# Three quarters of the feed-forward weights loaded beside the projections, the last one held back by an early logit, and the end of the first tile taken three steps at a time

## The chip, the cores and the metric

One NeuronCore of a Trainium2 chip runs the whole program. The metric is the device time of one execution in microseconds (us). A single core has no second die to compare with, so a run counts as slow only if it is over 1.5% above the fastest of the same kernel. Two runs are compared by ratio: the mean time of one kernel's fast runs over the mean of the other's fast runs of the same rounds on the same chip, with a 95% interval. That is not quite the ratio of the medians quoted beside it.

The profile names the engines PE (TensorE; PEld is its weight loads), DVE (VectorE), ACT (ScalarE), POOL (GpSimd) and SP (SyncE). A "q" behind a name (ACTq) is the issue of a DMA by that engine. "L947" is line 947 of the kernel shown. The changed kernel has more lines, so the same instruction has another number in it: the attention product is L1158 before and L1169 after, the gather L941 and L947.

## The reference, cut to what matters

```python
hs = layer_norm(h_source, ln1_scale, ln1_bias)        # h_source is x, 4096 x 512
ht = layer_norm(h_target, ln1_scale, ln1_bias)
q, k, v = ht @ Wq + bq, hs @ Wk + bk, hs @ Wv + bv    # 8 heads of 64; q scaled by 1/8
logits = where(adj != 0, q k^T, -1e30)                # adj: 4096 x 4096, about 0.4% ones
ctx = softmax(logits) @ v
ht = layer_norm(ht + ctx @ Wo + bo, ln2_scale, ln2_bias)
out = ht + gelu(ht @ W1) @ W2                         # W1 is 512 x 2048, W2 2048 x 512
return layer_norm(x + out)
```

The adjacency is sparse, some 16 neighbours to a row. The kernel therefore builds a list of neighbours per node, writes K and V to memory, and gathers the rows that a tile of 128 nodes needs.

## The kernel before

The program is written as Python generators that are woven together. The framework puts the result into one fixed order of instructions per engine at compile time. A "product" below is one attention product on VectorE, for up to three neighbours of each node of a tile; a "list block" is VectorE's work on one quarter of a tile's adjacency rows. Three stages follow each other and overlap: projections of x to K and V beside the building of neighbour lists from adjacency blocks; attention tile by tile (gathers by GpSimd, products and sums on VectorE); and the feed-forward part (FFN) of finished groups of tiles on TensorE beside the attention of later ones.

W1 and W2 are loaded in quarters. Two are loaded beside the projections. The other two come when the projections are done, into memory that the projections held:

```python
wp = mid.enter_context(tc.tile_pool(name="s1w", bufs=1, side="right"))   # holds R0, constants
...
def load_quarter(pool, q, engine=nc.sync):
    w1.append(pool.tile([P, KC, D], F32, name=f"w1_{q}"))
    w2.append(pool.tile([P, KC, D], F32, name=f"w2_{q}"))
    engine.dma_start(w1[q], W1[:, q * D:(q + 1) * D].rearrange("(c p) n -> p c n", p=P))
    engine.dma_start(w2[q], W2[q * D:(q + 1) * D, :].rearrange("(c p) n -> p c n", p=P))
...
                    if n in (8, 10):                    # pairs of projection tiles
                        load_quarter(wp2, n // 2 - 4)
...
            src.close()                                 # frees wk and wv
            mid.close()                                 # frees s1w, with the records R0
            pools = [late.enter_context(tc.tile_pool(name="s2wa", bufs=1)),
                     late.enter_context(tc.tile_pool(name="s2wb", bufs=1, side="right"))]
...
            def weights():
                for q, pool in enumerate(pools):
                    yield 10.0
                    load_quarter(pool, q + 2, nc.scalar)
```

Nodes are sorted by degree, and each node's *record* (its number, its degree, its list) is scattered to memory and read back tile by tile. Every gather needs a record; so does the output scatter, which writes a tile's finished rows to where the nodes belong. Seven buffers hold records:

```python
                rec = sp.tile([P, E0 + MAXE], I32, name="rec", bufs=7)
                eng = nc.gpsimd if i < 2 else nc.sync
                eng.dma_start(rec[:, :RW], recs_d[part][r0:r0 + P, :])
```

The end of a tile (normalising, its output matrix, the second layer norm, the transposes for the FFN) is a generator too, of which each call of `advance` takes one step, twice per group of logits:

```python
                def advance():
                    go_on()
                    for t in list(tails):
                        if next(t, StopIteration) is StopIteration:
                            tails.remove(t)
```

## Time and profile before

| | before |
|---|---|
| time, median of the first 3 runs (range) | 1874.8 us (1873.1 to 1874.85) |
| profiled execution, state fast | 1878.9 us, mean granted clock 0.960 |
| first attention product (of 211, counted from 0) | 315.8 us |
| first FFN matmul | 371.9 us |
| products 26 to 32 (from start to start) | 40.4 us |
| product 210, the last | 1739.5 us |

The prediction shows the page's shares and the table by stretch. Two further views also belong here. The first is the queue of SyncE's DMA issues by what it waited for (columns: line, releaser, us in total, times, longest). The loads of records (L955) wait again and again for an output scatter, because it is the last reader of a record's buffer:

```profile
SPq L955 <- DMA out_dram<-xt,rec: 958.9, 17, 103.8
```

The second is GpSimd's timeline around the first output scatter (start, duration, instruction; in brackets the idle time before it and what ended it):

```profile
491.28 1.03 POOL L1243 DMA_INDIRECT out_dram<-xt,rec  x1 [6.72 <-ACT xt L1239]
...
496.94 1.26 POOL L941 DMA_INDIRECT xt<-in_x_dram,rec  x1 [0.30 <-issue]
498.50 0.95 POOL L941 DMA_INDIRECT kv<-kvd,rec  x1 [0.30 <-issue]
...
511.06 0.95 POOL L941 DMA_INDIRECT tq<-in_L_gnn_h_target_dram,rec  x1 [2.70 <-PE t L1052]
```

GpSimd waits 6.72 us with the scatter, then gathers on without a stop, and fetches the rows of h_target for a later tile at 511.06, after 2.70 us of waiting. VectorE does not wait at all in that stretch: it is busy 19.98 of 20 us at 500 to 520.

### The profile page before, as it was taken

To read this page: it belongs to the slowest core of one execution; us is meant where nothing else is said; L and a number is where in the kernel's file an instruction comes from. 1 tells how busy PE (TensorE), PEld (TensorE's weight loads), DVE (VectorE), ACT (ScalarE), POOL (GpSimd) and SP (SyncE) were. 2 spreads that over 40 slices of the span, in tenths; PEclk is the share of its full clock that TensorE was granted. 3 is DMA by queue.
4 is the path that set the end of the run, shared out by engine and by line. 5 is a ranking of instruction groups with operands and counts; after the bars stand their busy time and mean duration, and the time that the engine had idled before them with its cause. 6 is when DMAs were issued, how large, how long until landed. Compare 5 with 4: busy or idle time off the path is not lost. (4 is left out here: it accounts for less than half of the span.)

```text
span 1878.9 us, 22938 instructions
## 1 busy us (share of the span) xinstructions
PE 1705.1 (91%) x7030; PEld 1100.5 (59%) x7030; DVE 1432.2 (76%) x2591; ACT 1247.5 (66%) x3139; POOL 885.2 (47%) x804
## 2 busy tenths in 40 slices
PE   7999784698998989999999989899999999999996
PEld 3444332565665656666666656566666666656664
DVE  7999855989998837787878889888777778777400
ACT  6777634577886737776777777677767677777411
POOL 1000143645445465656666666655555545655101
PEclk9999987698999989999999999999999999999998
DMA  9999958888887657777778778777677767666000
GB/s 349 381 380 360 353 167 332 314 273 299 313 271 246 207 158 230 257 252 263 251 253 276 271 269 293 241 246 246 216 239 232 248 224 237 227 220 223 23 1 24
DMA packets 147757, 463.28 MB, mean 247 GB/s; under 512 B 24468, under 2 KB 29160, under 8 KB 147624
## 3 DMA queue, kind: packets, MB, share of 16 engines
q0 software_dynamic: 95696, 342.19, 53.9%
q1 hardware_dynamic: 44112, 96.44, 14.5%
q10 hardware_dynamic: 7816, 23.08, 3.2%
q8 instruction: 58, 0.95, 0.2%
q14 instruction: 75, 0.61, 0.1%
HBM read 430.76 MB, written 30.89 MB: 246 GB/s over the span
## 5 line engine op out<-in xcount | busy, mean ns | idle before, releaser
L941 POOL DMA_INDIRECT kv<-kvd,rec x603 | 684.1, 1134 | 492.2 <-PE cps L1129 217.2
L1266 PE MATMUL pf<-h2T,w 128*128 128x256 f32 (+1 forms) x2176 | 475.9, 371 | 3.4 <-issue 2.6
L1275 PE MATMUL po<-w,gt 128*128 128x512 f32 x1024 | 469.4, 600 | 0.0
L1158 DVE TENSOR_TENSOR kv<-kv,tq 128x1536 f32<-128x1536 f32 (+2 forms) x211 | 352.6, 1677 | 107.2 <-DMA kv<-kvd,rec 84.5
L1266 PEld LDWEIGHTS pf<-h2T,w 128*128 128x128 f32 x2176 | 391.0, 193 | 68.8 <-issue 23.4
L1141 ACT ACTIVATE kv<-kv,pa 128x64 f32<-128x64 f32 x1520 | 391.5, 336 | 3.7
L1162 DVE TENSOR_REDUCE lg<-kv 128x24 f32<-128x1536 f32 (+2 forms) x211 | 351.0, 1670 | 1.8 <-ACT pa L1138 0.3
L1129 PE MATMUL cps<-ident,kv 128*128 128x128 f32 x2008 | 269.8, 282 | 52.9 <-DMA kv<-kvd,rec 20.4
L1129 PEld LDWEIGHTS cps<-ident,kv 128*128 128x128 f32 x2008 | 241.3, 146 | 129.2 <-issue 81.1
L1275 PEld LDWEIGHTS po<-w,gt 128*128 128x128 f32 x1024 | 188.3, 193 | 189.9 <-issue 189.0
L1121 DVE TENSOR_TENSOR kv<-kv,p 128x1024 f32<-128x1024 f32 (+1 forms) x211 | 249.9, 1191 | 47.4 <-ACT p L1166 30.3
L674 POOL TENSOR_TENSOR n_rs<-n_ve,mhalf 128x2 f32<-128x2 f32 (+2 forms) x51 | 51.3, 1005 | 333.8 <-DVE n_ve L667 136.7
L1269 ACT ACT_TABLE_LOAD x111 | 142.4, 1283 | 1.7
L980 PE MATMUL t<-wq,tq 128*128 128x512 f32 x256 | 119.9, 612 | 16.0 <-ACT tq L974 13.1
L906 PE MATMUL pq<-wk,h2T 128*128 128x512 f32 x256 | 124.0, 628 | 11.2 <-ACT h2T L896 5.8
L722 DVE MAX8 cand<-sg 128x8 uint16<-128x103 uint16 (+1 forms) x640 | 131.9, 257 | 0.7
L1269 ACT ACTIVATE gt<-pf 128x512 f32<-128x512 f32 x128 | 76.4, 597 | 72.5 <-PE pf L1266 60.8
L906 PE MATMUL pq<-wv,h2T 128*128 128x512 f32 x256 | 118.2, 604 | 6.0 <-ACT tq L908 5.9
L715 ACT ACTIVATE sg<-kv 128x1024 uint8<-128x1024 int32 x84 | 88.6, 1056 | 47.2 <-DVE cand L722 20.6
L1056 PE MATMUL t<-wo,rb 128*128 128x512 f32 x256 | 117.9, 604 | 1.5 <-DVE rb L1046 1.5
L906 PEld LDWEIGHTS pq<-wk,h2T 128*128 128x128 f32 x256 | 50.0, 202 | 78.2 <-issue 60.2
L1166 ACT ACTIVATE p<-lg 128x24 f32<-128x24 f32 (+2 forms) x179 | 33.7, 188 | 91.4 <-DVE lg L1162 69.9
(154 smaller groups left out, 1607.7 us busy)
## 6 DMA issues: line engine op xcount, KB each, us to landing
kv<-in_adj_dram SPq DMA_DIRECT2D x84, 512.0 KB
a<-in_adj_dram SPq DMA_DIRECT2D x44, 512.0 KB
kvd<-tq ACTq DMA_DIRECT2D x32, 512.0 KB
kv<-kvd,rec POOLq DMA_INDIRECT x603
kv<-in_L_gnn_h_target_dram SPq DMA_DIRECT2D x32, 256.0 KB
kv<-in_x_dram SPq DMA_DIRECT2D x15, 512.0 KB
rest_d<-gid SPq DMA_DIRECT2D x32, 160.0 KB
w<-in_L_gnn_W_dram SPq DMA_DIRECT2D x4, 1024.0 KB
```

Source lines behind the costliest of these rows:

```text
L722: nc.vector.max(cand[:, h * SQ + s, :], wd[:, w0:w1])
L906: nc.tensor.matmul(pkv, hT[:, kc, j * P:(j + 1) * P], w[:, kc, :], start=kc == 0, stop=kc == KC - 1)
L941: nc.gpsimd.indirect_dma_start(out=dst, out_offset=None, in_=table[:, :], in_offset=bass.IndirectOffsetOnAxis(ap=idx, axis=0))
L980: nc.tensor.matmul(pq, hT[:, kc, :], wq[:, kc, :], start=kc == 0, stop=kc == KC - 1)
L1121: nc.vector.tensor_tensor(v4, v4, p[:, j0:j0 + m, :].unsqueeze(3) .to_broadcast([P, m, H, HD]), ALU.mult)
L1129: nc.tensor.matmul(cps[:, c, :], kv[:, j, D + c * P:D + (c + 1) * P], ident, is_transpose=True, start=j0 + j == 0 and c == 0, stop=j0 + n ...
L1141: nc.scalar.mul(v, v, pa[:, hd:hd + 1])
L1158: nc.vector.tensor_tensor(kv[:, :n, :D], kv[:, :n, :D], tq[:, :D].unsqueeze(1).to_broadcast([P, n, D]), ALU.mult)
L1162: nc.vector.tensor_reduce(lg[:, :n, :], kv[:, :n, :D].rearrange("p j (h d) -> p j h d", h=H), AX.X, ALU.add)
L1266: nc.tensor.matmul(pf[:, k, :], w1[(f0 + k) // KC][:, kc, (f0 + k) % KC * P:((f0 + k) % KC + 1) * P], h2T[:, kc, :w], start=kc == 0, stop= ...
L1269: nc.scalar.activation(gt, pf, AF.Gelu_apprx_tanh)
L1275: nc.tensor.matmul(po[j], gt[:, k, j * P:(j + 1) * P], w2[(f0 + k) // KC][:, (f0 + k) % KC, :], start=False, stop=f0 + k == FC - 1, skip_g ...
```

## The change

The intent is to rid ScalarE of the wait of 14.20 us at the hand-over from projections to attention. Buffers of the early pools move into free slots of the gather ring, so that three quarters can be loaded beside the projections. The last quarter sits on wk and wv alone and is held by a logit of the second group. The end of the first tile goes three steps per call, so that its FFN starts while TensorE idles (in the kernel before it is busy 29.72 of 52 us at 320 to 372).

```diff
-            wp = mid.enter_context(tc.tile_pool(name="s1w", bufs=1, side="right"))
-            ip = mid.enter_context(tc.tile_pool(name="s1", bufs=2, side="right"))
+            words = ring[:, 7, :]                      # constants, moments (cut)
+            first_rec = ring[:, 11, :NA * RW].bitcast(I32).rearrange("p (n w) -> p n w", w=RW)
+            first_oh = ring[:, 11, 512:512 + NB * NA // 2].bitcast(BF16)
...
-            def load_quarter(pool, q, engine=nc.sync):
+            def load_quarter(pool, q, engine=nc.sync, gate=None):
...
+                if gate is not None:
+                    nc.scalar.copy(w1[q][:, 0, 0:1], gate)
+                    nc.scalar.copy(w2[q][:, 0, 0:1], gate)
...
-            DEEP = 8
+            DEEP = 7                                   # adjacency blocks ahead
...
-                return ring[:, DEEP + i // 2 % 4, i % 2 * D:(i % 2 + 1) * D]
+                return ring[:, 8 + i // 2 % 3, i % 2 * D:(i % 2 + 1) * D]
...
-                tails, pend = [], []
+                tails, pend, begun = [], [], set()
                 def advance():
                     go_on()
                     for t in list(tails):
-                        if next(t, StopIteration) is StopIteration:
-                            tails.remove(t)
+                        for _ in range(1 if h2Ts or begun else 3):
+                            if next(t, StopIteration) is StopIteration:
+                                tails.remove(t)
+                                break
+                    if h2Ts:
+                        begun.add(True)
...
+                            if k == 1:
+                                load_quarter(s2wa, NQ - 1, nc.scalar, lg[:, 0, 0:1])
...
-                    if n in (8, 10):
-                        load_quarter(wp2, n // 2 - 4)
+                    if n in (6, 8, 10):
+                        load_quarter(wp2, n // 2 - 3)
...
-            pools = [late.enter_context(tc.tile_pool(name="s2wa", bufs=1)),
-                     late.enter_context(tc.tile_pool(name="s2wb", bufs=1, side="right"))]
+            s2wa = late.enter_context(tc.tile_pool(name="s2wa", bufs=1))
...
-            def weights(): ...                         # two quarters after the projections
```

More of the change, by code (lines that the diff above doesn't have):

```diff
@@ L556, in adj_resnorm_kernel @@
             mid = ExitStack()
-            wp = mid.enter_context(tc.tile_pool(name="s1w", bufs=1, side="right"))
-            ip = mid.enter_context(tc.tile_pool(name="s1", bufs=2, side="right"))
             psi = mid.enter_context(tc.tile_pool(name="psi", bufs=1, space=PSUM))
             ring = kp.tile([P, RING, 2 * D], F32, name="kv")
+            words = ring[:, 7, :]
+            st, zero, bob, rbc = (words[:5 * KC, :P], words[:, 128:136], words[:, 136:136 + D],
+                                  words[:, 648:648 + KC])
+            mvh = words[:, 656:656 + 2 * NT].rearrange("p (n c) -> p n c", c=2)
+            veh, rsh, nmh = (words[:, 720 + i * NT:720 + i * NT + NT] for i in range(3))
+            first_rec = ring[:, 11, :NA * RW].bitcast(I32).rearrange("p (n w) -> p n w", w=RW)
+            first_oh = ring[:, 11, 512:512 + NB * NA // 2].bitcast(BF16)
             def xrows(n):
@@ L578, in adj_resnorm_kernel @@
                 nc.sync.dma_start(first_x[:, j, :], x[j * P:(j + 1) * P, :])
-            st = wp.tile([5 * KC, P], F32, name="st")
             for i, v in enumerate((ln1_scale, ln1_bias, ln2_scale, ln2_bias, bv)):
@@ L583, in adj_resnorm_kernel @@
             wv = load_w(kvw, Wv, "wv", nc.scalar)
-            Rs = [pool.tile([P, n, RW], I32, name=f"R{i}")
-                  for i, (pool, (_, n)) in enumerate(zip((wp, lp), PARTS))]
+            Rs = [first_rec, lp.tile([P, NBT, RW], I32, name="R1")]
             deg = lp.tile([P, NT], F32, name="deg")
@@ L625, in late_constants @@
             def late_constants():
-                zero = wp.tile([P, 2 * D // P], F32, name="zero")
                 nc.vector.memset(zero, 0.0)
@@ L632, in late_constants @@
                 nc.sync.dma_start(wq, Wq.rearrange("(c p) n -> p c n", p=P))
-                bob = row_bcast(wp, bo, "bob")
+                nc.sync.dma_start(bob, bass.AP(tensor=bo.tensor, offset=bo.offset,
+                                               ap=[[0, P], [1, D]]))
                 nc.sync.dma_start(bqr, bass.AP(tensor=bq.tensor, offset=bq.offset,
@@ L647, in late_constants @@
                                         ident)
-                rbc = wp.tile([P, KC], F32, name="rbc")
                 nc.vector.tensor_copy(rbc.unsqueeze(2), pt.rearrange("p (c t) -> p c t", c=KC)
@@ L688, in adj_resnorm_kernel @@
             held, moms = [], list(range(NT))
-            mvh = wp.tile([P, NT, 2], F32, name="mvh")
             adjs = []
-            DEEP = 8
+            DEEP = 7
             FILL = 5
@@ L791, in moments @@
                 t = hrow(i)
-                stats(ip, t, mvh[:, i, :], "n0")
+                stats(sp, t, mvh[:, i, :], "n2")
             def sort(part):
@@ L811, in sort @@
                 else:
-                    oh = wp.tile([P, NB * n], BF16, name="oh")
+                    oh = first_oh
                 oh = oh[:, :NB * n].rearrange("p (b i) -> p b i", b=NB)
@@ L868, in measure @@
                         return
-                    mv = ip.tile([P, G, 2], F32, name="mv")
+                    mv = sp.tile([P, G, 2], F32, name="mv2")
                     for j in range(G):
-                        stats(ip, state[n][:, j, :], mv[:, j, :], "n1")
-                    scales[n] = rstd_of(ip, mv, G, "n1")
+                        stats(sp, state[n][:, j, :], mv[:, j, :], "n2")
+                    scales[n] = rstd_of(sp, mv, G, "n2")
                 def scale(n):
@@ L1345, in prepare @@
                     moments(moms.pop(0))
-                rs, nm = rstd_of(wp, mvh, NT, "n0")
+                nc.vector.tensor_scalar_add(veh, mvh[:, :, 1], EPS)
+                nc.gpsimd.tensor_tensor(rsh, veh, mhalf, ALU.pow)
+                nc.vector.scalar_tensor_tensor(nmh, mvh[:, :, 0], -1.0, rsh, op0=ALU.mult,
+                                               op1=ALU.mult)
                 for R, (i0, n) in zip(Rs, PARTS):
                     Rf = R.bitcast(F32)
-                    nc.vector.tensor_copy(Rf[:, :, RST], rs[:, i0:i0 + n])
-                    nc.vector.tensor_copy(Rf[:, :, RST + 1], nm[:, i0:i0 + n])
+                    nc.vector.tensor_copy(Rf[:, :, RST], rsh[:, i0:i0 + n])
+                    nc.vector.tensor_copy(Rf[:, :, RST + 1], nmh[:, i0:i0 + n])
                 nm = lp.tile([P, QW], I32, name="a", bufs=2)
@@ L1369, in adj_resnorm_kernel @@
             mid.close()
-            pools = [late.enter_context(tc.tile_pool(name="s2wa", bufs=1)),
-                     late.enter_context(tc.tile_pool(name="s2wb", bufs=1, side="right"))]
+            s2wa = late.enter_context(tc.tile_pool(name="s2wa", bufs=1))
             psf = late.enter_context(tc.tile_pool(name="psf", bufs=2, space=PSUM))
-            def weights():
-                for q, pool in enumerate(pools):
-                    yield 10.0
-                    load_quarter(pool, q + 2, nc.scalar)
             def other_lists():
@@ L1384, in other_lists @@
                 yield from sort(1)
-            _weave((att, 0), (chain(feed(g) for g in range(len(GROUPS))), 0), (other_lists(), WAIT),
-                   (weights(), 0))
+            _weave((att, 0), (chain(feed(g) for g in range(len(GROUPS))), 0), (other_lists(), WAIT))
     left = nc.values_load(flag[0:1, 0:1], min_val=0, max_val=1)
```

## The prediction

> **What bounds the kernel now.** I read the busy shares by engine first, then the page's forty slices, then a table of busy times by stretch, and last the timeline of the stretch that looked thin. TensorE is busy for 91% of the span and VectorE for 76%, so the question is where TensorE is not busy, and whether what holds it there is something the change touches.
>
> ```profile
> PE 1705.1 (91%) x7030; PEld 1100.5 (59%) x7030; DVE 1432.2 (76%) x2591; ACT 1247.5 (66%) x3139; POOL 885.2 (47%) x804
> ...
> PE   7999784698998989999999989899999999999996
> ...
> PEclk9999987698999989999999999999999999999998
> DMA  9999958888887657777778778777677767666000
> ```
>
> The PE row drops to 4 and 6 tenths in slices 7 and 8 (47 us each, so 282 to 376 us), with the clock falling in slices 6 to 8. That stretch and a little before it in 20 us pieces; the columns are TensorE, its weight loads, VectorE, ScalarE and GpSimd busy us, then granted clock, DMA share and GB/s:
>
> ```profile
> 240.00:260.00 20.00, 20.00 (x61) 9.77 (x60) 18.58 (x73) 9.29 (x18) 12.13 (x12) 1.00 0.31 104
> 260.00:280.00 20.00, 14.28 (x29) 6.06 (x28) 3.52 (x16) 6.16 (x12) 9.30 (x11) 0.83 0.62 185
> 280.00:300.00 20.00, 13.49 (x31) 6.02 (x30) 8.67 (x35) 10.82 (x22) 0.00 (x0) 0.83 0.70 245
> 300.00:320.00 20.00, 5.46 (x13) 1.89 (x11) 10.37 (x27) 6.00 (x12) 11.10 (x11) 0.75 1.01 384
> 320.00:340.00 20.00, 9.00 (x39) 7.84 (x40) 19.64 (x25) 8.64 (x38) 16.03 (x14) 0.50 1.03 410
> 340.00:360.00 20.00, 14.37 (x62) 10.96 (x61) 18.74 (x21) 12.02 (x44) 13.31 (x12) 0.72 0.97 355
> ```
>
> Between 260 and 320 us nothing is full until the DMA at the end; from 320 us VectorE is full (attention on tile 0 plus lists) and TensorE half idle. So there are two stages: a hand-over from projections to attention that waits, and a VectorE-bound first attention tile. The timeline says what the hand-over waits for:
>
> ```profile
> 266.79 0.39 ACTq L573 DMA_DIRECT2D w<-in_L_gnn_W_dram  x1
> ...
> 267.28 0.58 ACT L908 COPY tq<-pq 128x512 f32<-128x512 f32 x1 [14.20 <-DMA rec<-R,ranki]
> ...
> 273.66 0.56 ACT L896 ACTIVATE h2T<-t,cols 128x256 f32<-128x256 f32 x1 [4.69 <-DMA w<-in_L_gnn_W_dram]
> ...
> 283.22 0.81 ACT L967 ACTIVATE tq<-tq,rec 128x512 f32<-128x512 f32 x1 [5.04 <-DMA tq<-in_L_gnn_h_target_dram,rec]
> ...
> 299.55 0.33 ACTq L910 DMA_DIRECT2D kvd<-tq  x1
> ...
> 299.90 0.46 ACTq L574 DMA_DIRECT2D w<-in_L_gnn_W_dram  x1
> ...
> 305.85 0.94 POOL L941 DMA_INDIRECT kv<-kvd,rec  x1 [26.39 <-issue]
> ...
> 315.82 1.76 DVE L1158 TENSOR_TENSOR kv<-kv,tq 128x1536 f32<-128x1536 f32 x1 [4.30 <-DMA kv<-kvd,rec]
> ```
>
> Read from the top: ScalarE stands for 14.2 us ahead of evicting a projection. What released it is the scatter of the records, and the first thing it did then was to issue a weight quarter. The last quarter of W1 and W2 lies on the bytes of the records R0 (pool "s1w"), so its load, issued from ScalarE in program order, holds every ScalarE instruction behind it until the scatter has read R0. Then 4.7 us more for a weight DMA. The last K/V write goes out at 299.55, quarter 2 straddles it, the first K/V gather follows at 305.85, and attention starts at 315.8.
>
> [...] the rate in this trace, 368 GB/s in the first 100 us with many transfers in flight, decides, and makes a quarter (two transfers of 1.05 MB) 5.7 us. [...]
>
> **The change part by part.**
>
> Removed: the ScalarE wait. The four projection tiles still open at 251 us write K/V at 273, 277, 290 and 300 us. By TensorE a tile costs 16 matmuls, 3.6 us per eight, and 1.2 us of transposes: 8.4 us, so four cost 34 us and would end at about 285 us instead of 299.
>
> Added: a third quarter beside the projections (at the sixth pair of tiles, about 115 us). That stage has a DMA share of 0.98 to 1.0, so its 2.1 MB are not free. The two quarters already loaded there, issued at 150.8 and 185.7 us, are each followed by a wait of the list stage for adjacency rows:
>
> ```profile
> 167.62 1.06 ACT L715 ACTIVATE sg<-kv 128x1024 uint8<-128x1024 int32 x1 [3.56 <-DMA kv<-in_adj_dram]
> ...
> 201.15 1.06 ACT L715 ACTIVATE sg<-kv 128x1024 uint8<-128x1024 int32 x1 [7.56 <-DMA kv<-in_adj_dram]
> ```
>
> Their mean, 5.6 us, is what the transfer takes, so I charge 5 us. DEEP from 8 to 7 takes one prefetched block of seven away and may make each such wait a little longer; I put that in the range. The moved buffers (records, constants, one-hot) lie in ring slots 7 and 11, which the third and fourth gather group fill long after their last reading; no new wait.
>
> When can attention start? Two chains must both end. *Records*: the scatter started at 244.5; plus 5 is 249.5; its 16 instructions took 21 us: 270.5; records back, 8 us before with a weight quarter ahead of them, 5 estimated: 275.5; two x gathers, 2.6 us, go first: 278; the h gather, 7.4 us before, say 6: 284; front end (scale 0.8, transposes 1.1, copies 1.5, eight matmuls 3.7, bias 0.7, hops between) 10 us where it took 19 among blocked evictions: 294. *Projections*: 285 plus about 2 of the DMA delay, 4 us until the last write has landed (6.3 before): 291; the first three gathers, 3.8 us to issue and 3 to land: 298. So attention starts at about 299 us, 17 us earlier than 315.8.
>
> Moved: the last quarter to ScalarE at the second group of logits, held there by two one-element copies (about 0.2 us each). It now sits on wk and wv only, which are free by then. It competes with gathers at a DMA share near 1; before, quarter 2 was moved at the same time, so the bytes after 296 us are the same, but now they come behind the first gathers instead of ahead of them. VectorE may wait up to one quarter's 5.7 us; I charge 2.
>
> Three steps at a time: tile 0's end runs from its first VectorE step to the first FFN matmul as
>
> ```profile
> 339.29 0.24 DVE L1026 SCALAR_TENSOR_TENSOR pm<-rec,p 128x88 f32<-128x88 int32 x1
> ...
> 371.86 0.80 PE L1266 MATMUL pf<-h2T,w 128*128 128x128 f32 x2
> ```
>
> 32.6 us, for twelve steps of which two are taken per group of logits. With three at a time it is four calls, two groups, or some 10 us, but the dependent work itself (four ScalarE passes, 4 us of matmuls, a 2 us power on GpSimd) is about 15 us. So the FFN of group 0 starts some 15 us sooner against attention, into a TensorE that is only 29.7 of 52 us busy at 320 to 372. That group's FFN is a single tile and the next group's cannot start before its own normalised rows exist, so the last FFN does not come earlier by this; it only takes about 15 us of TensorE work out of 372 to 440, where VectorE loses time. VectorE is busy 94.8 of 108 us at 372 to 480; I give a third of the 13 us back, 4, and take 1 for waits inside the squeezed end.
>
> Sum: 17 - 2 + 4 - 1 = 18 us, 1874.8 - 18 = 1856.8, so 1857.
>
> Does the gain last? From 480 to 580 VectorE is 99% busy, and from 700 to 1760 TensorE is busy 1012 of 1060 us: stages with no slack, in a fixed order, so they move as a block.
>
> **The rivals.** (a) *The DMA takes it back*: the early stage is bound by the DMA, and a third quarter, shallower prefetch and a late quarter among the gathers eat 12 us or more. For it: shares of 1.0 and the 7.6 us wait. Against: the share is only 0.31 at 240 to 260 and 0.62 at 260 to 280, so the delay is partly caught up there. It would give 1868 to 1875. (b) *The records become the bound*: projections finish early and attention waits for scatter and front end, as slow as before. For it: h rows landed only at 283 and the scatter starts 5 us later. This gives a start near 306 and 1864. (c) *The early FFN counts in full*: all of TensorE's idle 52 us at 240 to 400 is filled and none is lost later. For it: TensorE sets the end. Against: VectorE is full from 320 on and the FFN of group 1 waits for attention. It would give 1830 to 1838.
>
> **Range and chances.** The start of attention is uncertain by about 7 us, the two smaller terms by 4 each, later re-timing by 4: 1842 to 1868 for 8 in 10. Over 2% faster means below 1837.3, which needs (c): 0.08. Slower than 1912 needs a fresh stall that I don't see: 0.02. Within 2%: 0.90.
>
> **What would show it.** No ScalarE wait above 5 us between 250 and 285; last K/V write near 287; first attention product near 299; first FFN matmul near 340, that is 40 us after it where it was 56; an adjacency wait of 4 to 7 us after 115 us and scatter near 249. I am wrong if attention starts later than 308 (rival a or b), or if the gain at the end differs by over 8 us from that at the start of attention.

## The result, and the profile after

The changed kernel took 1891.21 us (median of 4 runs, 1890.34 to 1892.88) against 1873.95 us (1871.41 to 1874.85) of the kernel before on the same chip: ratio 1.0095 [1.0078, 1.0113]. It is about 0.9% slower, where 1% faster was predicted. Both profiled executions are of state fast, 1888.8 us at a clock of 0.961 and 1878.9 us at 0.960, so the clock explains nothing. I show the rows of the changed kernel's page that answer to those in the prediction:

```profile
PE 1701.8 (90%) x7030; PEld 1097.7 (58%) x7030; DVE 1431.7 (76%) x2591; ACT 1240.2 (66%) x3135; POOL 884.7 (47%) x804
...
PE   7999883778899989999999989999999999999996
...
PEclk9999987898989999999999999999999999999998
DMA  9999958977767556777878888867667767766000
```

The work per engine is the same within 4 us, ScalarE's within 8 (1240.2 against 1247.5); it is its place that differs. The table by stretch (columns as in the prediction) has the hand-over no shorter to speak of, and attention on tile 0 as thin as before:

```profile
240.00:260.00 20.00, 20.00 (x60) 9.78 (x59) 19.74 (x86) 12.82 (x24) 13.25 (x13) 1.00 0.48 170
260.00:280.00 20.00, 13.89 (x32) 5.82 (x31) 6.40 (x27) 5.75 (x11) 8.60 (x10) 0.91 0.61 179
280.00:300.00 20.00, 16.32 (x33) 6.80 (x34) 15.39 (x63) 12.77 (x26) 0.00 (x0) 0.84 0.74 247
300.00:320.00 20.00, 1.72 (x4) 0.38 (x2) 11.76 (x29) 8.46 (x22) 15.49 (x14) 0.67 0.94 354
320.00:340.00 20.00, 7.10 (x31) 6.33 (x32) 17.57 (x21) 7.47 (x33) 9.86 (x10) 0.50 1.03 404
```

To see where time is lost, I read from both traces when each attention product starts. The lag is the start after minus the start before, so negative is ahead:

| product | 0 | 8 | 10 | 14 | 22 | 26 | 28 | 30 | 32 | 42 | 100 | 150 | 210 |
|---|---|---|---|---|---|---|---|---|---|---|---|---|---|
| lag, us | -4.1 | -0.1 | 21.1 | 11.9 | -6.6 | -5.5 | 3.2 | 15.9 | 14.5 | 12.2 | 15.6 | 14.2 | 9.9 |

There are three events. At the start only 4 us were won. Between products 8 and 10 some 21 us go, and by product 22 they are back, with 7 us on top. Between products 26 and 32 another 20 us go (60.4 us where the kernel before took 40.4), and most of these are never paid back: from 5.5 us ahead at product 26 the kernel falls to 9.9 us behind at the last, which is the whole difference of the two profiled executions.

**The hand-over.** The timeline of the changed kernel:

```profile
265.42 0.38 SPq L1214 DMA_DIRECT2D degs<-rec  x1
...
268.34 0.33 ACTq L916 DMA_DIRECT2D kvd<-tq  x1
...
268.71 0.56 ACT L902 ACTIVATE h2T<-t,cols 128x256 f32<-128x256 f32 x1 [9.89 <-DMA degs<-rec]
...
278.38 0.81 ACT L973 ACTIVATE tq<-tq,rec 128x512 f32<-128x512 f32 x1 [1.40 <-DMA tq<-in_L_gnn_h_target_dram,rec]
...
293.35 0.33 ACTq L916 DMA_DIRECT2D kvd<-tq  x1
...
300.15 0.94 POOL L947 DMA_INDIRECT kv<-kvd,rec  x1 [26.42 <-DMA kvd<-tq]
...
311.76 1.76 DVE L1169 TENSOR_TENSOR kv<-kv,tq 128x1536 f32<-128x1536 f32 x1 [4.64 <-DMA kv<-kvd,rec]
```

The 14.2 us wait of ScalarE is gone, and 9.89 us stand in its place. What released ScalarE was the load of the degrees (`degs`), which ScalarE has no use for. That load, used only in a check at the very end, had been hoisted to here and, by the view of SyncE's waits, stood 17.6 us for the record scatter before it went out at 265.42. The K/V write of 268.34 came after it; in e3 below, with the load moved to the end, the write went out at 260.28. Why the write was held by a load whose data it does not use is not shown. So the change removed one wait for the scatter and uncovered another.

**The first stop.** With three steps per call the first FFN matmul comes at 360.93 instead of 371.86, and its work stands in TensorE's order ahead of the matmuls of tile 2's query (tiles counted from 0), which begin at 368.98 instead of 354.12. Product 9, the first of that tile, needs the query:

```profile
360.93 0.67 PE L1280 MATMUL pf<-h2T,w 128*128 128x128 f32 x4
...
368.98 3.60 PE L986 MATMUL t<-wq,tq 128*128 128x512 f32 x8
...
377.00 0.42 DVE L726 TENSOR_TENSOR sg<-sg,lio 128x512 uint16<-128x512 uint16 x1 [4.28 <-ACT sg L721]
...
381.40 0.68 DVE L988 SCALAR_TENSOR_TENSOR tq<-t,bqr 128x512 f32<-128x512 f32 x1
...
382.21 1.09 POOL L947 DMA_INDIRECT kv<-kvd,rec  x1 [12.24 <-PE cps L1140]
382.40 3.42 DVE L1169 TENSOR_TENSOR kv<-kv,tq 128x1536 f32<-128x1536 f32 x2
```

TensorE has finished these matmuls by 372.6, but VectorE finishes the query (L988) only at 381.40: its order has list blocks (L726) first, and they wait for ScalarE. GpSimd waits 12.24 us for transposes of tile 1 meanwhile, but with a gather for a later product; the rows of product 9 had been asked for by 348. VectorE does six list blocks from 360 to 382 us without one attention product. Those lists would have had to be built later anyway, which is why this stop is paid back: by product 10 the changed kernel has begun 105 blocks against 94, by product 26 both have begun 112.

**The second stop.** The 20 us stretches of both kernels, before first, with VectorE in the third pair of columns after the two of TensorE:

```profile
500.00:520.00 20.00, 18.54 (x83) 12.51 (x82) 19.98 (x45) 17.75 (x50) 11.45 (x11) 1.00 1.00 374
520.00:540.00 20.00, 19.29 (x80) 11.84 (x79) 20.00 (x45) 15.90 (x37) 9.49 (x7) 1.00 0.88 304
```

```profile
500.00:520.00 20.00, 12.14 (x49) 7.49 (x47) 11.56 (x25) 9.23 (x28) 8.67 (x10) 0.88 0.82 310
520.00:540.00 20.00, 17.11 (x61) 10.68 (x62) 17.09 (x68) 13.90 (x23) 5.75 (x6) 0.78 0.68 220
```

All engines do less in the same 20 us: TensorE 12.14 us for 18.54, VectorE 11.56 for 19.98. Here every engine waits for another, and the view of waits from 490 to 545 us of the changed kernel gives its links (us in total, times, longest):

```profile
POOL tq L947 <- PE t L1058: 12.9, 1, 12.9
ACT p L1177 <- DVE lg L1173: 10.7, 1, 10.7
POOL kv L947 <- PE cps L1140: 9.7, 4, 5.1
DVE kv L1169 <- DMA kv<-kvd,rec: 8.8, 2, 8.4
PEld t L1058 <- ACT tq L980: 8.3, 1, 8.3
```

Its beginning is seen on GpSimd:

```profile
486.49 2.12 POOL L1257 DMA_INDIRECT out_dram<-xt,rec  x1 [6.66 <-ACT xt L1253]
...
493.51 0.96 POOL L947 DMA_INDIRECT xt<-in_x_dram,rec  x1 [1.13 <-DMA out_dram<-xt,rec]
498.41 1.75 POOL L947 DMA_INDIRECT kv<-kvd,rec  x1 [3.94 <-DMA rec<-rec]
...
524.28 1.19 POOL L947 DMA_INDIRECT tq<-in_L_gnn_h_target_dram,rec  x1 [12.88 <-PE t L1058]
```

The scatter itself waits as long as before (6.66 and 6.72 us). But the gather behind the fetch of x rows now waits 3.94 us for a record, whose buffer the scatter had just read. VectorE then stands 8.44 us for a gather, ScalarE for VectorE, TensorE for ScalarE, and GpSimd, at 524.28, for TensorE. The fetch that came at 511.06 before comes 13 us later.

That fetch is for tile 7, whose first product is 36. What product 30, the first of tile 6, follows by 1 us in both kernels is its own query, here the changed kernel and then the kernel before:

```profile
521.34 1.50 ACT L980 ACTIVATE tq<-t,b1r,cols 128x128 f32<-128x128 f32 x4
538.71 0.68 DVE L988 SCALAR_TENSOR_TENSOR tq<-t,bqr 128x512 f32<-128x512 f32 x1
```

```profile
508.58 1.50 ACT L974 ACTIVATE tq<-t,b1r,cols 128x128 f32<-128x128 f32 x4
522.98 0.69 DVE L982 SCALAR_TENSOR_TENSOR tq<-t,bqr 128x512 f32<-128x512 f32 x1
```

In the changed kernel ScalarE has that step of the query behind the 10.7 us wait of the view above. VectorE's order differs too: ten list blocks begin between products 26 and 32, where the kernel before has six, and VectorE is busy 47.6 of the 60.4 us against all of the 40.4. So some 7 of the 20 us are list work moved forward, and 13 are idle. It is still a loss: from product 26 to 42 both kernels do sixteen list blocks and VectorE is busy about as long (117.1 and 116.1 us), yet the changed kernel takes 143.3 us and the one before 125.6.

### The profile page after: what moved, and what is told of

The parts are those of the page before. It is cut to its first block, busy times and chain, and to the rows that moved or that the text cites. A ratio compares the mean times of both kernels' runs of the same rounds, so it can differ in the third digit from the quotient of the medians.

```text
span 1888.8 us, 22937 instructions
## 1 busy us (share of the span) xinstructions
PE 1701.8 (90%) x7030; PEld 1097.7 (58%) x7030; DVE 1431.7 (76%) x2591; ACT 1240.2 (66%) x3135; POOL 884.7 (47%) x804
## 5 line engine op out<-in xcount | busy, mean ns | idle before, releaser
L1140 PE MATMUL cps<-ident,kv 128*128 128x128 f32 x2008 | 264.3, 280 | 59.0 <-DVE kv L1132 43.8
L681 POOL TENSOR_TENSOR n_rs<-n_ve,mhalf 128x2 f32<-128x2 f32 (+1 forms) x50 | 42.9, 859 | 330.1 <-DVE n_ve L674 123.1
L1062 PE MATMUL t<-wo,rb 128*128 128x512 f32 x256 | 124.8, 633 | 2.3 <-DVE rb L1052 2.3
```

What stands on the lines that cost most here:

```text
L1062: nc.tensor.matmul(pa, ct[:, c, :], wo[:, c, :], start=False, stop=c == KC - 1, skip_group_check=True)
L1140: nc.tensor.matmul(cps[:, c, :], kv[:, j, D + c * P:D + (c + 1) * P], ident, is_transpose=True, start=j0 + j == 0 and c == 0, stop=j0 + n ...
```

## The experiments

All ratios are to the kernel before, from the fast runs of the same rounds. "8 to 10" and "26 to 32" are us between the starts of those products in the run's profile; 10.4 and 40.4 is the kernel before. Each is read from one profiled execution, while the ratio is over all fast runs, and the two need not go together: e6 and e18 have long second stops at small ratios.

| run | base and edit | median us | ratio [95%] | product 0 | 8 to 10 | 26 to 32 |
|---|---|---|---|---|---|---|
| e1_one_step | after, one step per call | 1894.22 | 1.0088 [1.0061, 1.0115] | 313.1 | 10.4 | 58.9 |
| e2_three_only | before, three steps per call | 1879.71 | 1.0014 [1.0002, 1.0026] | 315.4 | 34.4 | 43.4 |
| e3_degs_late | after, degrees loaded at the end | 1886.93 | 1.0052 [1.0035, 1.0068] | 312.5 | 33.3 | 56.6 |
| e4_one_step_degs_late | e1 and e3 | 1894.67 | 1.0083 [1.0054, 1.0113] | 308.9 | 10.2 | 60.1 |
| e5_handover_free | e3, six records loaded by GpSimd | 1887.54 | 1.0045 [1.0028, 1.0063] | 311.4 | 32.7 | 58.8 |
| e6_eight_records | after, eight record buffers | 1878.74 | 1.0015 [0.9996, 1.0034] | 313.3 | 32.5 | 54.8 |
| e7_two_late | after, two early and two late quarters | 1892.47 | 1.0081 [1.0056, 1.0106] | 314.8 | 30.9 | 56.6 |
| e8_depth_seven | before, seven blocks ahead | 1884.19 | 1.0029 [1.0015, 1.0042] | 319.7 | 10.2 | 41.4 |
| e9_wind_first | after, first group finished early | 1893.12 | 1.0062 [1.0041, 1.0083] | 314.7 | 32.9 | 53.4 |
| e10_wind_eight | e9 and e6 | 1888.27 | 1.0041 [1.0020, 1.0063] | 314.3 | 32.2 | 51.8 |
| e11_before_eight | before, eight record buffers | 1870.75 | 0.9952 [0.9938, 0.9967] | 316.3 | 9.7 | 40.4 |
| e12_before_wind | before, first group finished early | 1876.41 | 0.9979 [0.9969, 0.9989] | 319.4 | 9.7 | 40.6 |
| e13_last_woven | after, last quarter's place as before | 1878.90 | 1.0014 [0.9997, 1.0030] | 313.1 | 22.7 | 49.4 |
| e14_last_woven_eight | e13 and e6 | 1875.52 | 0.9992 [0.9982, 1.0002] | 317.0 | 21.5 | 46.1 |
| e15_three_eight | e2 and e11 | 1877.21 | 1.0001 [0.9985, 1.0016] | 319.5 | 34.1 | 43.7 |
| e16_before_wind_eight | e12 and e11 | 1870.28 | 0.9953 [0.9936, 0.9971] | 321.9 | 10.2 | 40.5 |
| e17_last_first_logits | after, last quarter at group 0 | 1882.70 | 1.0017 [1.0004, 1.0029] | 312.0 | 30.7 | 48.3 |
| e18_last_fourth_logits | after, last quarter at group 3 | 1886.49 | 1.0045 [1.0031, 1.0059] | 315.1 | 33.3 | 58.7 |

The runs came in five jobs; the kernel before had medians between 1876.85 and 1880.40 us in them (1873.95 in the first comparison), so medians of different jobs are not compared. The changed kernel was not run again in them: its 1.0095 rests on four runs of each kernel.

### The three steps: with and without

```diff
-                        for _ in range(1 if h2Ts or begun else 3):
+                        for _ in range(1):
```

> The changed kernel with the first tile's end back at one step a call; the loads stay as changed. Squeezed-end theory (the three steps alone put first-FFN and list work ahead of tile 2's attention in the fixed engine orders, which cost 21 us at attention group 10 and some 20 us again near 500 us): groups 8 to 10 take about 10 us instead of 31, and the whole is about 1870 us, a little under the kernel before. Load theory (more bytes in the early stage, shallower prefetch, a late quarter among the gathers cost it): stays at 1888 to 1894 us.

The other way round, the kernel before with that loop alone:

> The kernel before with the three steps alone; all loads as before. Squeezed-end theory: 1885 to 1892 us, with the stop of attention at groups 8 to 12 in its trace. Load theory: 1872 to 1877 us.

Without the three steps the first stop is gone (10.4 us) and the time stays at 1.0088: the second stop is still 58.9 us. With the three steps alone the first stop is there in full (34.4 us), the second hardly (43.4), and the cost is 0.1%. So the three steps make the first stop, nearly all of it is paid back, and the loss that lasts is not theirs.

### The hand-over: one wait behind another

In the check at the end, a copy that needs the end's sums keeps the degrees' load from being hoisted:

```diff
+                    nc.vector.tensor_copy(degs[:, i0:i0 + n, 0], ok[:, i0:i0 + n])
                     nc.sync.dma_start(degs[:, i0:i0 + n, :], rec...)
```

> The changed kernel, with the load of the degrees for the final verdict tied to the end of attention by a small copy into its tile, so that it cannot be hoisted into the hand-over. Lane theory (the K/V write of the fourth tile from the end waits for the degrees' load [...], and that load waits for the record scatter): the 9.9 us ScalarE wait before 268 us goes, the last K/V write goes out at 283 to 288 instead of 293 and attention starts near 304 instead of 311.8; the end is 4 to 8 us earlier if no order changes. Rival (the true need is the records and the front end): attention starts within 2 us of 311.8.

The same with one step per call:

> Both edits together. If both theories hold: attention starts near 304, no stop at groups 8 to 12, and 1858 to 1866 us, faster than both kernels. If only the squeezed-end theory holds: about 1870. If neither: 1888 to 1894.

In e3 the K/V write of 268.34 went out at 260.28. Yet ScalarE then stood 10.51 us, now for adjacency rows:

```profile
274.15 1.06 ACT L721 ACTIVATE sg<-a 128x1024 uint8<-128x1024 int32 x1 [10.51 <-DMA a<-in_adj_dram]
```

In the changed kernel's trace such loads (L706, from 269.69) stand in SyncE's queue behind the loads of records 2 to 5 (L961, from 265.85), which go out after the 17.6 us wait for the scatter; that it is the same in e3 was the author's estimate. The next run takes these record loads off SyncE too, issuing them from GpSimd, which waits for the scatter anyway (1.76 us in e3):

```diff
-                eng = nc.gpsimd if i < 2 else nc.sync
+                eng = nc.gpsimd if i < 6 else nc.sync
```

> The changed kernel with the degrees' load tied to the end (as in the run before) and the record loads of tiles 2 to 5 issued from GpSimd instead of SyncE, so that no queue but GpSimd's holds an instruction that waits for the record scatter. Queue theory ([...] taking one away only uncovers the next): no ScalarE wait over 5 us from 255 to 276, last K/V write at 280 to 288 instead of 293, attention starts at 298 to 306. Rival (the records' own chain, scatter to record to h row to query, sets the start): attention starts at 309 to 313 as before. The end moves by no more than 8 us either way, since the second loss near 500 us is untouched.

```profile
271.06 1.06 ACT L721 ACTIVATE sg<-a 128x1024 uint8<-128x1024 int32 x1 [8.68 <-DMA a<-in_adj_dram]
...
278.46 0.81 ACT L973 ACTIVATE tq<-tq,rec 128x512 f32<-128x512 f32 x1 [6.26 <-DMA tq<-in_L_gnn_h_target_dram,rec]
```

Attention starts at 311.4 us in e5, against 311.8 with all waits in place; 8.68 us for adjacency rows and 6.26 us for the rows of h_target are there now. Three times a ScalarE wait of 9 to 14 us was taken away, and the start moved by 4 us in all. So it is not one ScalarE wait that sets it. The traces point to the fixed order in which the last projection tiles and the first query tiles share TensorE and ScalarE, the latter waiting for the record scatter; no run changed that order alone, so this is not shown. The end moved by 0.4 to 0.5% in e3 and e5, though not through the start; e4, which starts earliest (308.9), gained nothing.

### The early quarter and the prefetch depth

Two quarters beside the projections, as before, and two held by the second group's logit:

```diff
-                    if n in (6, 8, 10):
-                        load_quarter(wp2, n // 2 - 3)
+                    if n in (8, 10):
+                        load_quarter(wp2, n // 2 - 4)
...
                             if k == 1:
+                                load_quarter(wp2, NQ - 2, nc.scalar, lg[:, 0, 0:1])
```

> The changed kernel with two quarters beside the projections, at the same places as before, and two at the first logits. Byte theory (the third quarter in the full early stage costs about 5 us there): scatter 4 to 6 us earlier, attention starts 3 to 6 us earlier, and with 2 MB more behind the first logits groups 2 to 8 take up to 6 us longer; end within 5 us of the changed kernel unless the order near group 28 changes.

And `DEEP = 7` alone in the kernel before:

> The kernel before with the adjacency prefetch at seven blocks instead of eight and nothing else. If the shallower prefetch costs the early stage: scatter and start of attention 3 us or more later, 1877 to 1883 us. If not: within 2 us of the kernel before.

A second late quarter in place of the third early one changes nothing that the intervals could tell (1.0081, 56.6 us). The expectation missed: the scatter came at 249.14 instead of 243.10, and attention started 3 us later, not earlier. Since e7 both takes a quarter away early and adds one late, it does not clear the early quarter by itself; e13 below, which keeps it and stands at 1.0014, level with e2, does. `DEEP = 7` costs the kernel before 0.3% with no stop of either kind; its attention starts at 319.7 us.

### The record buffers

```diff
-                rec = sp.tile([P, E0 + MAXE], I32, name="rec", bufs=7)
+                rec = sp.tile([P, E0 + MAXE], I32, name="rec", bufs=8)
```

> The changed kernel with eight record buffers instead of seven, so that the record of the eighth tile need not wait until the first tile's output scatter has read its own. Record theory (the loss of some 20 us between attention groups 26 and 30 starts with that wait: a gather put early in GpSimd's order stands 3.9 us for it, and VectorE, ScalarE and TensorE follow in turn): groups 26 to 30 take 32 to 40 us instead of 54, and the end is 1872 to 1881 us. Rival (the stretch is slow because of the order of the engines' queues as a whole): 48 us or more, end 1888 to 1896.

> Control: the kernel before with eight record buffers. If the record wait is a cost that the change brought in: within 3 us of the kernel before. If eight buffers are simply a gain of their own, which the change had no part in: 5 us or more faster, about 1868.

Eight buffers take the changed kernel from 1.0095 to 1.0015. But the kernel before gains 0.5% by them too, and 1.0015 over 0.9952 is 1.0063: two thirds of the change's cost remain when both have eight. In the changed kernel the six products still take 54.8 us, although the wait for the record is gone. In the two profiles e6 is 6 us ahead of the changed kernel at product 32 and 13 us at the last, so about half of the gain lies there or earlier. In e11 nothing is gained by product 32 and 12 us by the last. SyncE's queue in e11, against the 958.9 us of before:

```profile
SPq L955 <- DMA out_dram<-xt,rec: 658.6, 15, 87.0
```

In the changed kernel that total is 996.0 us and in e6 996.4, no shorter, so the sum of these waits does not explain what eight buffers are worth there.

### The end of the first group, wound up early

If the place of the first output scatter is what hurts, finishing the first group at once should help:

```diff
-                if g + 1 == len(GROUPS):
+                if g in (0, len(GROUPS) - 1):
                     while ends: wind_up()
```

> The changed kernel, with the end of the first group (normalisation and output scatter) finished right after its FFN instead of step by step beside the next group's FFN; seven record buffers. In its GpSimd order the first output scatter moves from behind gather 78 to behind gather 48. Scatter-place theory (the stretch of groups 26 to 32 is lost because GpSimd stands 6.7 us at that scatter, and then at a gather for the record that the scatter frees, with the gathers of the next groups behind it): groups 26 to 32 take 40 to 45 us (61 in the changed kernel, 40 in the one before), end 1873 to 1880. Rival (the order of the other engines near there is to blame): 55 us or more there, end 1886 to 1893.

> Both repairs: first group's end finished at once, and eight record buffers. If the two losses are different waits of the record buffers (the first near 500 us, others later), they add: 1868 to 1875, at or below the kernel before; if the one contains the other, within 3 us of the better of the two.

> Control: the kernel before with the first group's end finished at once. Its stretch of groups 26 to 32 takes 40 us already, so within 3 us of the kernel before if the place of the scatter did no harm there; 5 us or more faster if it did.

> The kernel before with eight record buffers and the first group's end wound up right after its feed-forward part. If the two gains add: 0.9952 times 0.9979, ratio 0.993, 1861 to 1868 us. If they are two ways to the same 5 us: 0.995 to 0.996, level with eight buffers alone.

On the changed kernel both runs, e9 and e10, missed. In e9 the scatter moved from behind 78 gathers to behind 48 in GpSimd's order, but the six products took 53.4 and 51.8 us and the ratios were 1.0062 and 1.0041. The place of this one scatter is thus not the cause by itself. In the kernel before, the same edit gives 0.2% alone and nothing on top of eight buffers (0.9953 and 0.9952): two ways to the same gain.

### The last quarter's place

What was left untested was where the last quarter stands. First it goes back to where the kernel before has its late loads, right after the projections and without the copies that hold it; all else of the change stays:

```diff
-                            if k == 1:
-                                load_quarter(s2wa, NQ - 1, nc.scalar, lg[:, 0, 0:1])
...
+            def weights():
+                yield 10.0
+                load_quarter(s2wa, NQ - 1, nc.scalar)
```

> The kernel after, with only the last quarter's load put back where the kernel before has its late loads (issued from ScalarE right after the projections in program order, with no copy of a logit to hold it). Theory A (the place of the last quarter, at the second group of logits, re-timed the engines' orders at the 26th to 32nd attention product): those six products take 40 to 46 us, as with three steps alone, and the ratio to before is 1.001 to 1.004. Theory B (the cause lies in what stays of the change: the third early quarter, seven blocks of prefetch, buffers moved to the gather ring, one buffer less for the moments): they take 55 to 62 us and the ratio stays 1.007 to 1.011.

> The same as the run before it with eight record buffers. Theory A: level with the kernel before with eight record buffers, ratio 0.995 to 0.998. Theory B: as the kernel after with eight, ratio 1.000 to 1.003, with 50 us or more for the six products.

> The kernel before with three steps at a time and eight record buffers, nothing of the loads changed. If the three steps cost nothing at the end and the buffers' gain adds to it: ratio 0.9952 times 1.0014, 0.995 to 0.998, with 36 to 44 us for the 26th to 32nd attention product. If three steps and the shortage of record buffers act together, eight buffers would bring it below the kernel before with eight: under 0.994.

The ratio falls from 1.0095 to 1.0014, as theory A had it, level with three steps alone. The six products take 49.4 us, between what A and B expected; 11 of the 20 us are back at this spot, and from product 30 on the run is some 12 us ahead of the changed kernel. GpSimd in e13:

```profile
483.25 1.03 POOL L1254 DMA_INDIRECT out_dram<-xt,rec  x1 [0.31 <-issue]
491.96 0.97 POOL L947 DMA_INDIRECT xt<-in_x_dram,rec  x1 [7.67 <-DMA out_dram<-xt,rec]
493.24 0.94 POOL L947 DMA_INDIRECT kv<-kvd,rec  x1 [0.30 <-issue]
...
512.36 0.95 POOL L947 DMA_INDIRECT tq<-in_L_gnn_h_target_dram,rec  x1 [4.72 <-DVE kv L1169]
```

The scatter does not wait, the gather behind the x rows comes at 493.24 instead of 498.41, and the fetch that stood 12.88 us before 524.28 comes at 512.36. With eight buffers it makes 0.9992, not the 0.995 to 0.998 expected; and e15 with 1.0001 missed its 0.995 to 0.998 as well. So an eighth buffer is worth 0.8% in the changed kernel (1.0095 to 1.0015), 0.5% in the kernel before, and 0.2% or less in e13 and e2 (1.0014 to 0.9992 and 1.0001). Its worth depends on the order it meets; the reason is not shown. Compared like with like, e14 against e15, the changed loads without the hold are worth 0.1%, within the intervals.

A quarter on its way among the first gathers and an order of queues that comes out otherwise both fit so far. Two runs tell them apart. GpSimd's compiled order has the first output scatter behind 81 gathers in before, e2 and e13, and behind 78 in the changed kernel. Holding the last quarter by group 0 gives 81, by group 3 gives 78:

```diff
-                            if k == 1:
+                            if k == 0:         # e17;  k == 3 in e18
```

> The kernel after, with the last quarter held by a logit of the first group instead of the second. Its transfer starts some 5 us earlier, still among the first gathers, but in the fixed order of GpSimd the first output scatter stands behind 81 gathers, as in the kernels that do not lose time there. Theory A1 (what costs is the order of the queues that the place of this load leads to, 160 us later): ratio 1.000 to 1.004, 42 to 50 us for the 26th to 32nd attention product. Theory A2 (what costs is the hold itself, a transfer that starts while the first tiles gather): ratio 1.007 to 1.011, and 55 us or more.

> The kernel after, with the last quarter held by a logit of the fourth group. In GpSimd's order the first output scatter stands behind 78 gathers, as in the kernel after. Theory A1: the loss between the 26th and 32nd product stays, 54 us or more, ratio 1.006 to 1.011. Theory A2: as bad or worse, since the transfer comes later still; so this run tells the two apart only together with the one before it. If it is level with the kernel before (below 1.004), the place of the scatter is not what counts.

When the quarter went out, first in e17, then in e18 (in the changed kernel it was 321.64):

```profile
315.89 0.39 ACTq L583 DMA_DIRECT2D w<-in_L_gnn_W_dram  x1
```

```profile
333.92 0.39 ACTq L583 DMA_DIRECT2D w<-in_L_gnn_W_dram  x1
```

And GpSimd, again e17 first:

```profile
487.93 1.03 POOL L1257 DMA_INDIRECT out_dram<-xt,rec  x1 [0.53 <-ACT pa L1149]
...
515.91 0.95 POOL L947 DMA_INDIRECT tq<-in_L_gnn_h_target_dram,rec  x1 [6.75 <-DVE cand L728]
```

```profile
485.10 1.94 POOL L1257 DMA_INDIRECT out_dram<-xt,rec  x1 [7.83 <-ACT xt L1253]
...
520.97 0.95 POOL L947 DMA_INDIRECT tq<-in_L_gnn_h_target_dram,rec  x1 [10.82 <-DVE cand L728]
```

The same load, held the same way among the first gathers and issued 5.75 us earlier, costs 0.0017 instead of 0.0095, with 48.3 us for the six products. Issued 12 us later it brings the second stop back, 58.7 us, at the ratio 1.0045, less than expected. (The profiled executions flatter this contrast: e17's took 1879.37 us, below its median, and e18's 1891.41 us, above it.) The transfer as such is therefore not what costs: of the two transfers issued from 321.64 us on, the one whose landing is in the trace took 12.2 us, some 150 us before the stop, and the cost does not grow with the time of issue. What is left is the order of the queues that the place of the load leads to at compile time. How much of the 0.0095 that order makes is less sure: e18 has the same place of the scatter and nearly the same stop at half the cost.

## Why the prediction was wrong

- **The wait at the hand-over.** It rightly saw the 14.2 us wait, and that the change removes it. It was worth 17 us in the sum and brought 4. The record path was even better than predicted: scatter at 243.1 us (249.5 predicted), query rows at 278.4 (284). The projections path failed: the last K/V write came at 293.35 us, not 287, behind the 9.89 us wait for the degrees' load; and from the first gather to the first product it took 11.6 us (300.15 to 311.76) where 6.8 were put down. The trace of before had 10.0 there (305.85 to 315.82); I should have used it. Rival (b), records as the bound with a start near 306, came nearest in time but not in its mechanism: tile 0's query was there by 296.3 us (294 predicted), and the first K/V gather, at 300.15, was released by the last K/V write. e3 and e5 show that no single ScalarE wait set that.
- **The third early quarter.** The step charged 5 us. A wait of 4.72 us did follow that load, at 136 us, but the scatter started 1.4 us earlier than before, not 5 later: it was caught up by then. e7 and e13 give no sign of a cost at the end. The shallower prefetch, left to the range, costs the kernel before 0.3% by itself (e8), about 5 us; that it costs as much within the change is not shown. Rival (a), the DMA taking the gain back, fell for the early stage.
- **The last quarter.** It was charged 2 us, for VectorE waiting while the transfer runs. This is the mis-sized term: by e13 its place costs about 0.8% (1.0095 less 1.0014), some 15 us. The mechanism was wrong too: not the transfer beside the gathers but, by e17 and e18, the order of queues 160 us later.
- **Three steps.** Put at plus 4 less 1. The FFN did start earlier (360.93, predicted near 340), but ahead of tile 2's query in TensorE's order and with list blocks ahead of it in VectorE's, which stopped attention for 21 us. The stop was paid back in list work, so the net is 0.1% lost (e2).
- **"They move as a block."** This is the step that failed most. Attention started 4 us ahead and was still 5.5 us ahead at product 26, so the sum to there had only its sizes wrong. Then 20 us were lost in the very stretch that I called 99% busy and without slack. A stage without slack can still lose, and here it lost because the fixed orders were no longer the same orders: ten list blocks instead of six between those products, and the query of tile 6 at 538.71 us instead of 522.98. The prediction named "later re-timing by 4" as a margin; it was 20 there and 15 at the end. That the loss at the end (17 us by the medians) is about as large as the gain that was forecast is chance.

What stays open: why the scheduler puts the scatter and the fetches where it does, and which link of the new order is decisive. The scatter's place marks the slow orders (75 to 79 gathers ahead: 54.8 to 60.4 us, in the changed kernel, e1, e3 to e7 and e18; 81 or 82: 40.4 to 49.4, in the kernel before, e2, e8, e11, e13 to e15 and e17), but e9 shows that moving it alone does not cure them.

## What to carry to other kernels

Before taking a wait away, list what the same engine would wait for next: the next load behind the same event, and any late load that the engine is released by without using its data (here 14.20 us gave way to 9.89 us for the degrees, and these to 10.51 us for adjacency rows). Where a scheduler fixes the order at compile time, moving a load is two edits, the transfer and a new order for every queue; put the load at two or three neighbouring places and look at all of them before believing a cause, since here one group of logits earlier was worth 0.8%. A buffer whose last reader is a late output can set the pace of the loads that reuse it: with one more record buffer the waits of such loads fell from 958.9 to 658.6 us in the kernel before, and it was 0.5% faster (ratio 0.9952), the best version found together with e16 (0.9953), faster than both kernels of this study.
